# A one-core attention and FFN kernel: 64-row shift transposes at a unit's head, V tiles in first blocks, and a last chunk in three tiles and one

## The chip, the core and the metric

The kernel runs on one core of a Trainium2 chip. The metric is the device time of one execution in microseconds, the median of several runs; before the change it is 2961.74 us (three runs, 2959.02 to 2964.38).

## The reference

The input x has shape [2, 2048, 256] in float32. Attention and FFN each have a norm on both sides, and each is of the form x + layernorm(layer(layernorm(x))):

```python
x = x + _layernorm(_L0_attn_ref(_layernorm(x), Wq, bq, Wk, bk, Wv, bv, Wo, bo, gamma, beta))
x = x + _layernorm(_L0_ffn_ref(_layernorm(x), w_gate, w_up, w_down))
```

`_L0_attn_ref` is 16-head attention with 64 elements a head: projections with biases, softmax(q k / 8) v, an output projection with bias, the residual, and a layer norm with gamma and beta. `_L0_ffn_ref` has integer weights scaled by 1/127: silu(x Wg) * (x Wu), 768 hidden elements, and then the product with Wd.

## The kernel before, in words

**Units.** Attention is cut into 64 units (b, p, c): batch b of 2, head pair p of 8, block c of 512 queries of 4. `run_unit` runs one of them, in two blocks j = 0 and 1 of eight key tiles (128 keys each). For each key tile it issues the pair of products that gives the scores' maxima of the *next* unit (`max_pair`, L625, and DVE's reduction L632), and then the scores of this one (`scores`, L663): three pairs of float32r products (high by high, high by low, low by high) and a fourth pair, `unit` by `SH[u]`, that subtracts the row's shift; ScalarE takes the exponential (L664). Each head of the pair uses 64 rows of the array, so the shape of these products is 64\*128 (rows by columns) and they come in pairs. After a block follow the output projection of the unit before (`wo_half`, L252, with DVE's accumulation L263), POOL's and DVE's sums of the exponentials (`add_up`, L674 to L684), side jobs, and the eight PV steps (`pv`, L694), whose shape is 128\*64. In block 0 `sum_up` (L199) and the copy `first_half` (L223) come behind; then SyncE moves the row sums with eight small transfers (`few`, L208).

**The shift.** `shift_min` (DVE, L635) leaves the minima of the next unit's maxima in `n8`, columns 0 and 64. `shift_row` (L639) transposes its four 128x128 tiles on TensorE (L643) and ScalarE copies the result to `SH` (L645). In the kernel before, `run_unit` calls `shift_row(ahead)` behind block 1's PV steps; `cs_item(u)` follows it: DVE adds the two PV halves to `cf` (L230), ScalarE copies it to the high part of `cs` (L232), and POOL takes the low part (L233).

**What sets the order.** TensorE, DVE, ScalarE and POOL run in the order in which the program issues (`manual_schedule`); SyncE's transfers are ordered by the framework's scheduler. Side jobs are generators: `items(g)` says which begin in which block, and `advance` moves each one step when its kind, "R" (before PV's side work) or "F" (side work on TensorE), comes up. Before the change, "R" and "F" come up in both blocks. F jobs are the projections (`projs`, L578), V tiles (`v_tile`, L603, 24 products and a DVE add L613), weight preparation in batch 0 (`prep_jobs`, transposes L340), x transposes for batch 1 (`next_x`, `x_item`, L553 to L558), and the head jobs in batch 1 that turn finished attention rows of batch 0 into FFN input (`head_job`, L278 to L323, transposes L315).

**Buffers.** PSUM has two double buffers with tag "t" (`double()`: scores, projections, V, transposes, `wo_half`) and two with tag "x" (maxima and PV). There are 9 buffers for exponentials and 5 for V tiles.

**FFN.** Eight chunks of 512 rows, six hidden blocks each (`gate_up`, L961 to L983). A slot is one `gate_up` and one step of each waiting job: `end_job` (down products L995 of the chunk before, its norm and output), `own_job` (the norms of batch 1's rows), `x_out` (transposes L955 and the split L186, L187 of the next chunk, for chunks 4 to 7), and `last_units` (what attention left open). `finish` ends the last chunk.

Of the kernel before, what the change touches and what calls it, by code (L numbers as in the profile page):

```python
# [16 lines left out]
P = 128  # L17
# [11 lines left out]
def kernel(  # L29
# [112 lines left out]
    def x_chunk(b, c):  # L142
        return x_like(x, b, c)
# [83 lines left out]
    def cs_item(u):  # L227

        f = op.tile([P, QB], F32, tag="cf", name="cf")
        nc.vector.tensor_tensor(f, pvs.pop(u)[:, 0, :], raws.pop(u), ALU.add)  # L230
        t = op.tile([P, 2, QB], F32R, tag="cs", name="cs", bufs=2)
        nc.scalar.copy(t[:, 0], f)  # L232
        nc.gpsimd.tensor_tensor(t[:, 1], f, f32(t[:, 0]), ALU.subtract)  # L233
        ctxs[u] = t
# [92 lines left out]
    def prep_jobs():  # L327
        jobs = []

        def piece(w, dst, o, i0):  # L330
            src = hd.tile([P, TT, D], F32, tag="hx", name="wi")[:, 0, :].bitcast(I32)
            nc.sync.dma_start(out=src, in_=w[o * P : (o + 1) * P, i0 * P : (i0 + 2) * P])
            yield "R"
            f = hd.tile([P, TT, D], F32, tag="hy", name="wf")[:, 0, :]
            nc.scalar.copy(f, src)
            yield "F"
            yield "F"
            ps = double()[:, 0, :]
            for i in range(2):
                nc.tensor.transpose(ps[:, i * P : (i + 1) * P], f[:, i * P : (i + 1) * P], ident)  # L340
            t = hd.tile([P, TT, D], F32, tag="ht", name="wt")[:, :2, :].bitcast(F32R)
            split(t, ps[:, : 2 * P])
            for k in range(2):
                nc.sync.dma_start(
                    out=dst[:, k, i0 : i0 + 2, o * P : (o + 1) * P],
                    in_=f32(t[:, k, :]).rearrange("p (i n) -> p i n", i=2),
                )

        for w, dst, no, ni in (
            (w_gate, wg_dram, HC, DC),  # L350
            (w_up, wu_dram, HC, DC),
            (w_down, wd_dram, DC, HC),
        ):
            for o in range(no):
                for i0 in range(0, ni, 2):
                    jobs.append(piece(w, dst, o, i0))
        return jobs
# [87 lines left out]
    with ExitStack() as actx:  # L445
# [113 lines left out]

        def next_x(b, c):  # L560

            t = x_load(b, c)
            yield "R"
            x_norm(b, c, t)
            yield "F"
            x_item(c, t)
# [71 lines left out]

        def shift_row(u):  # L639

            ps = double()[:, 0, :]
            for qt in range(QT):
                nc.tensor.transpose(ps[:, qt * P : (qt + 1) * P], n8[:, qt, :], ident)  # L643
            SH[u] = bw.tile([P, QB], F32R, tag="sh", name="sh", bufs=2)
            nc.scalar.copy(SH[u], ps)  # L645

        def scores(u, kt):

# [55 lines left out]
        def items(g):  # L704

            b, p, c = units[g]
            at = {}

            def put(j, kind, f, *a, late=False):
                at.setdefault((j, kind), []).append((late, lambda: f(*a)))  # L710

            def now(j, f, *a):


                def job():
                    f(*a)
                    yield from ()

                put(j, "F", job)

            left = len(units) - g
            if p == 0:
                put(0, "R", next_acc, b, c)
            if b == 0 and p and (c != 2 or p == 1) and prep:
                put(0, "R", lambda: prep.pop(0), late=True)
            if b == 1 and 4 * p + c in (5, 11, 17, 23):
                put(0, "R", head_job, 0, (5, 11, 17, 23).index(4 * p + c), nc.gpsimd, late=True)
            if left == 3:
                put(1, "R", load_ffn, 0)
            if left == 2:  # L730
                put(0, "R", load_ffn, 1)
                put(1, "R", load_ffn, 2)
            if left == 1:
                put(0, "R", load_ffn, 3)
            if left == 2:
                put(1, "R", ahead, late=True)
            if b == 0 and p == 0:

                put(0, "R", x_stats_item, 1, c, late=True)


            want = [(0, *units[g + 2])] if left > 2 else []
            nb, npair = (b, p + 1) if p + 1 < NP else (b + 1, 0)
            if nb < B:
                same = nb == b
                want += [
                    (1, nb, npair, i)
                    for i in {1: (0,) if same else (), 2: (1,) if same else (0, 1), 3: (2, 3)}.get(c, ())
                ]
            for i in range(0, len(want), 2):  # L750
                now(0, projs, *want[i : i + 2])
            if c == 0 and p % 2 == 0:

                if g:
                    now(0, v_tile, b, p // 2, 3)
            if nb == B:
                return at
            if c == 0:
                put(0, "R", load_w, 1, nb, npair)
            if c == 1:  # L760
                put(0, "R", load_w, 0, nb, npair)
            if c == 2:
                put(0, "R", load_wo, nb, npair)
            if nb != b and c < 2:
                put(0, "R", next_x, nb, 2 * c)
                put(1, "R", next_x, nb, 2 * c + 1)
            if npair % 2 == 0:
                pg = npair // 2
                if c == 0:
                    put(1, "R", load_wv, nb, pg)  # L770
                if c == 2:
                    now(1, v_tile, nb, pg, 0)
                if c == 3:
                    now(1, v_tile, nb, pg, 1)
                    now(1, v_tile, nb, pg, 2)
            return at

        def begin():
# [64 lines left out]
            maxima(15, 16)  # L843
            shift_min(first)
            v_tile(0, 0, 3, True)
            shift_row(first)
            drain(load_wo(0, 0))

        ahead_job = own_job(OWN)
# [1 line left out]
        def ahead():  # L851
            for _ in ahead_job:
                yield "R"

        running = []

        def advance(kind, new):
# [9 lines left out]

        def run_unit(g, u):
            at = items(g)
            ahead = units[g + 1] if g + 1 < len(units) else None  # L870
            behind = units[g - 1] if g else None
            for j in range(2):
                for i in range(8):
                    if ahead and i < 7:
                        max_pair(ahead, 8 * j + i)
                    scores(u, 8 * j + i)
                if ahead:
                    max_pair(ahead, 8 * j + 7)
                if j == 1:
                    if ahead:  # L880
                        shift_min(ahead)
                    if behind:
                        inv_item(behind)


                if j == 1 and behind:
                    wo_half(behind, 0)
                if j == 0 and g > 1:
                    wo_half(units[g - 2], 1)
                adding = add_up(u, j)  # L890
                next(adding, None)
                advance("R", at.get((j, "R"), []))
                if j == 0:
                    advance("F", at.get((j, "F"), []))
                for i in range(8):
                    pv(u, 8 * j + i)
                if j == 0:
                    if behind:
                        sum_up(behind, pvs[u][:, 1, :])
                    first_half(u, behind)  # L900
                else:
                    if ahead:
                        shift_row(ahead)
                    cs_item(u)
                    drain(adding)
                    advance("F", at.get((j, "F"), []))

        with tc.manual_schedule(engines={EV.PE, EV.DVE, EV.Activation, EV.Pool}):
            begin()
# [135 lines left out]

    def finish(ch):

        mv = end_mv()
        for i in range(TT):
            down(ch, i, range(HC - 1))  # L1050
        for i in range(TT):
            down(ch, i, range(HC - 1, HC))
            end_stats(ch, i, mv)
        ready = end_rstd(mv)
        for i in range(0, TT, 2):
            end_out(ch, i, *ready, nc.vector)

    def last_units():

        wo_half(units[-2], 1)  # L1060
        yield
        ps = bank()
        sum_up(last, ps)
        row = op.tile([P, 2, QB], F32, tag="rr", name="rr")[:, 0, :]
        nc.scalar.copy(row, ps)
        sum_rows(last, row)
        for _ in range(3):
            yield
        inv_item(last)
        yield  # L1070
        wo_half(last, 0)
        yield
        wo_half(last, 1)

# [7 lines left out]
    with tc.manual_schedule(engines={EV.PE, EV.DVE, EV.Activation, EV.Pool}):  # L1082
        ffn_load(0)
        ffn_load(1)
        for ch in range(len(chunks)):
            for hc in range(HC):
# [5 lines left out]
                    jobs.append(own_job(OWN_AT[n]))  # L1092
                if ch > 0 and hc == 1:
                    jobs.insert(0, end_job(ch - 1))
                if hc == 3 and OWN <= ch + 1 < len(chunks):
                    jobs.append(x_out(ch + 1))
                for j in list(jobs):
                    if next(j, j) is j:
# [54 lines left out]
```

## Time and profile before

| | before |
|---|---|
| median of three runs | 2961.74 us |
| the profiled execution | 2966.69 us |
| its span, first to last instruction | 2964.9 us |
| mean granted TensorE clock | 0.995 |
| POOL's sums of exponentials, L677 | 636 x 2546 ns |
| DVE's maxima, L632 | 1024 x 1225 ns |
| exponentials, L664 | 1024 x 1027 ns |
| shift transposes, L643 | 256 x 286 ns (median 273) |
| shift copies, L645 | 64 x 588 ns |
| cs: DVE's add L230, ScalarE's copy L232, POOL's subtraction L233 | medians 692, 622, 1294 ns |

In the profile's rows the first number is the start in us from the span's start, then the length, the engine, the line, the operation, the tiles written and read, the shape (for TensorE first the part of the array that is used, rows\*columns) and the count. In brackets stands the idle time before, and what ended it. Matmul records overlap each other, since the array is pipelined, so that the step from one start to the next says more than the length of a record. The name s stands for both maxima and PV, t for every tile of the tag "t".

### The profile page before, as it was taken

To read this page: it belongs to the slowest core of one execution; us is meant where nothing else is said; L and a number is where in the kernel's file an instruction comes from. 1 tells how busy PE (TensorE), PEld (TensorE's weight loads), DVE (VectorE), ACT (ScalarE), POOL (GpSimd) and SP (SyncE) were. 2 spreads that over 40 slices of the span, in tenths; PEclk is the share of its full clock that TensorE was granted. 3 is DMA by queue.
4 is the path that set the end of the run, shared out by engine and by line. 5 is a ranking of instruction groups with operands and counts; after the bars stand their busy time and mean duration, and the time that the engine had idled before them with its cause. 6 is when DMAs were issued, how large, how long until landed. Compare 5 with 4: busy or idle time off the path is not lost.

```text
span 2964.9 us, 48241 instructions
## 1 busy us (share of the span) xinstructions
PE 2891.5 (98%) x19236; PEld 1749.7 (59%) x19236; DVE 2081.5 (70%) x2689; ACT 1466.1 (49%) x1740; POOL 2442.2 (82%) x1396
## 2 busy tenths in 40 slices
PE   7999999999999999999999999999999999999998
PEld 5555565556555565556555655555555565555887
DVE  6776677776777767776777777776777667774663
ACT  4545444554455444554555545454545445554443
POOL 4999878887888878887899988899799889988553
PEclk9999999999999999999999999999999999999999
DMA  2000000000000000010000001001000000112000
GB/s 59 19 12 12 13 12 12 10 17 5 15 12 13 10 12 24 5 42 10 26 21 10 7 10 33 5 13 31 5 7 24 20 1 10 44 58 72 29 29 29
DMA packets 125394, 59.10 MB, mean 20 GB/s; under 512 B 77200, under 2 KB 118416, under 8 KB 124784
## 3 DMA queue, kind: packets, MB, share of 16 engines
q1 hardware_dynamic: 124960, 55.62, 7.0%
q8 instruction: 150, 2.46, 0.3%
q0 software_dynamic: 208, 0.40, 0.1%
q14 instruction: 76, 0.62, 0.1%
HBM read 37.89 MB, written 17.83 MB: 19 GB/s over the span
## 4 chain that ended last, share of the span: by engine, by line
PE 83%; POOL 8%; DVE 4%; ACT 3%; issue 2%; DMA 1%; SPq 0%; ACTq 0%; POOLq 0%; DVEq 0%
PE t L663 29%; PE s L694 27%; PE s L625 8%; POOL accs L677 5%; PE t L578 5%; PE t L603 3%; ACT pt L664 2%; PE fp L995 2%; PE up L968 2%; PE gp L968 2%; PE s L199 2%; PE t L252 1%; PE t L643 1%; DVE nm L632 1%; POOL accs L684 1%
## 5 line engine op out<-in xcount | busy, mean ns | idle before, releaser
L677 POOL TENSOR_TENSOR accs<-accs,pt 128x1024 f32<-128x1024 f32 x636 | 1619.4, 2546 | 273.2 <-ACT pt L664 228.1
L632 DVE TENSOR_REDUCE nm<-s 128x2 f32<-128x1024 f32 x1024 | 1216.1, 1225 | 508.6 <-PE s L625 507.8
L664 ACT ACTIVATE pt<-t 128x1024 f32<-128x1024 f32 x1024 | 1050.0, 1027 | 258.6 <-PE t L663 188.0
L663 PE MATMUL t<-QN,KT 64*128 64x512 f32 x6144 | 915.5, 403 | 5.5 <-ACT pt L664 2.8
L694 PE MATMUL s<-pt,v 128*64 128x512 f32 x4096 | 907.1, 595 | 0.0
L663 PEld LDWEIGHTS t<-QN,KT 64*128 64x128 f32 x6144 | 522.6, 185 | 241.2 <-ACT pt L664 171.8
L694 PEld LDWEIGHTS s<-pt,v 128*64 128x64 f32 x4096 | 282.8, 137 | 538.1 <-issue 525.9
L625 PE MATMUL s<-KT,QN 64*128 64x512 f32 x2048 | 422.2, 409 | 6.5 <-DVE cf L230 3.7
L663 PE MATMUL t<-sh,unit 64*128 64x512 f32 x2048 | 405.5, 392 | 0.0
L684 POOL TENSOR_TENSOR accs<-accs,two 128x1024 f32<-128x1024 f32 x128 | 305.3, 2385 | 18.7 <-DVE two L683 7.7
L681 DVE TENSOR_TENSOR two<-pt 128x1024 f32<-128x1024 f32 x128 | 290.5, 2269 | 0.0
L625 PEld LDWEIGHTS s<-KT,QN 64*128 64x128 f32 x2048 | 192.1, 184 | 128.0 <-issue 61.1
L223 ACT COPY rr<-s 128x1024 f32<-128x1024 f32 x63 | 64.0, 1015 | 393.5 <-PE s L199 386.3
L645 ACT CAST sh<-t 128x512 fp32r<-128x512 f32 x64 | 37.6, 588 | 434.9 <-PE t L643 434.9
L263 DVE SCALAR_TENSOR_TENSOR acc<-t,rc,acc 128x256 f32<-128x256 f32 x500 | 206.9, 477 | 20.0 <-PE t L252 13.2
L663 PEld LDWEIGHTS t<-sh,unit 64*128 64x128 f32 x2048 | 193.4, 185 | 45.2 <-ACT sh L645 0.2
L674 POOL TENSOR_TENSOR accs<-pt 128x1024 f32<-128x1024 f32 x64 | 155.5, 2430 | 47.3 <-ACT pt L664 46.9
L578 PE MATMUL t<-xh,wqk 128*128 128x512 f32 x512 | 181.2, 414 | 12.5 <-ACT pt L664 10.5
L982 POOL TENSOR_TENSOR hT<-hf,hT 128x512 fp32r<-128x512 f32 x48 | 61.9, 1289 | 106.5 <-ACT hT L981 106.5
L578 PEld LDWEIGHTS t<-xh,wqk 128*128 128x128 f32 x512 | 97.7, 191 | 47.1 <-ACT pt L664 23.4
L588 ACT ACTIVATE QN<-t,bq_sb 128x512 fp32r<-128x512 f32 x64 | 44.0, 688 | 148.7 <-PE t L578 148.6
L252 PE MATMUL t<-wo,cs 64*128 64x256 f32 x1500 | 114.7, 285 | 1.6 <-ACT pt L664 1.5
(163 smaller groups left out, 2177.7 us busy)
## 6 DMA issues: line engine op xcount, KB each, us to landing
few<-rr SPq DMA_DIRECT2D x512, 0.5 KB, 2.0
xc<-in_L_attn_x_dram SPq DMA_DIRECT2D x8, 512.0 KB, 4.0
xT_dram<-hn SPq DMA_DIRECT2D x16, 256.0 KB, 2.2
out_dram<-o SPq DMA_DIRECT2D x16, 256.0 KB, 2.2
xT<-xT_dram SPq DMA_DIRECT2D x3, 1024.0 KB, 5.9
attn_dram<-acc SPq DMA_DIRECT2D x5, 512.0 KB, 2.6
acc<-in_L_attn_x_dram SPq DMA_DIRECT2D x4, 512.0 KB, 8.8
raw_w<-in_L_attn_Wq_dram SPq DMA_DIRECT2D x16, 128.0 KB, 2.2
```

The source lines that it names most:

```text
L252: nc.tensor.matmul(ps[e][:, i * D : (i + 1) * D], t[half(e), ci, s], w[half(e), wi, :], start=k == 0, stop=k == 2,)
L263: nc.vector.scalar_tensor_tensor(a, ps[e][:, i * D : (i + 1) * D], inv[:, e, q : q + 1], a, ALU.mult, ALU.add)
L578: nc.tensor.matmul(ps[:, k, :], w[:, wi, dc, :], xx[:, dc, s], start=n == 0, stop=n == 5)
L625: nc.tensor.matmul(s[:, e, :], QN[u][half(e), 0, qt * P : (qt + 1) * P], KT[b, p, kc][half(e), 0, :], start=True, stop=True,)
L632: nc.vector.tensor_reduce(nm[u][:, :, qt, kc : kc + 1], s, AX.X, ALU.max, negate=True)
L663: nc.tensor.matmul(ps[:, e, :], w, r, start=n == 0, stop=n == 3)
L664: nc.scalar.activation(pt, ps, AF.Exp, scale=QSCALE)
L674: nc.gpsimd.tensor_tensor(accs[u], todo[0], todo[1], ALU.add)
L677: nc.gpsimd.tensor_tensor(accs[u], accs[u], t, ALU.add)
L681: nc.vector.tensor_tensor(two, p8[n], p8[n + 1], ALU.add)
L684: nc.gpsimd.tensor_tensor(accs[u], accs[u], two, ALU.add)
L694: nc.tensor.matmul(pvs[u][half(e), 0, :], v[:, kt % 4, n : n + K], pt[:, e, :], start=kt % 8 == 0, stop=kt % 8 == 7,)
```

## The change

It has these parts.

1. `shift_row(u)` is called at the head of unit u and no longer behind the block before it. Each 128x128 transpose becomes two of 64 rows, one per half of `n8`'s partitions, which write 64 columns each in two banks; ScalarE's copy gathers from both.
2. `cs_item` stops after DVE's add. Its ScalarE copy and POOL subtraction are issued at the head of the next unit, behind the shift's copy. Behind the last unit they are issued at once.
3. "F" comes up in block 0 alone. V tile 0 of the next pair stays in unit c = 2, now in block 0; tiles 1 to 3 are made in block 0 of unit c = 0. Weight preparation loses one of its two "F" waits.
4. `next_x` gets a tile of its own for each of the chunks 0 to 2 (chunk 3 shares with 0), and chunk 1 begins in block 0 of its unit.
5. Head jobs 2 and 4 begin a unit earlier (11 to 10, 23 to 22).
6. FFN: `x_out` begins at hidden block 1 and not 3. In `last_units` the reciprocal and the first half of the projection come one slot earlier; the second half stays in its slot.
7. `finish` runs the first three tiles to their end, starts their norm, runs the fourth tile's 18 products, and writes four tiles of 128 rows each, not two of 256.

```diff
         nc.vector.tensor_tensor(f, pvs.pop(u)[:, 0, :], raws.pop(u), ALU.add)
+        yield
         t = op.tile([P, 2, QB], F32R, tag="cs", name="cs", bufs=2)
...
             nc.scalar.copy(f, src)
             yield "F"
-            yield "F"
...
-            t = x_load(b, c)
+            t = hd.tile([P, TT, D], F32, tag=("hx", "hy", "ht", "hx")[c], name="xc")
+            nc.sync.dma_start(out=t, in_=x_chunk(b, c))
...
-            ps = double()[:, 0, :]
+            ps = double()
             for qt in range(QT):
-                nc.tensor.transpose(ps[:, qt * P : (qt + 1) * P], n8[:, qt, :], ident)
+                for h in range(2):
+                    nc.tensor.transpose(
+                        ps[:, h, qt * K : (qt + 1) * K], n8[half(h), qt, :], ident[half(h), half(h)]
+                    )
             SH[u] = bw.tile([P, QB], F32R, tag="sh", name="sh", bufs=2)
-            nc.scalar.copy(SH[u], ps)
+            nc.scalar.copy(
+                SH[u].rearrange("p (q h r) -> p h q r", h=2, r=K),
+                ps[:, :, : QT * K].rearrange("p h (q r) -> p h q r", r=K),
+            )
...
-            if b == 1 and 4 * p + c in (5, 11, 17, 23):
-                put(0, "R", head_job, 0, (5, 11, 17, 23).index(4 * p + c), nc.gpsimd, late=True)
+            if b == 1 and 4 * p + c in (5, 10, 17, 22):
+                put(0, "R", head_job, 0, (5, 10, 17, 22).index(4 * p + c), nc.gpsimd, late=True)
...
-                if g:
-                    now(0, v_tile, b, p // 2, 3)
+                for i in range(1, 4) if g else ():
+                    now(v_tile, b, p // 2, i)
...
-                put(1, "R", next_x, nb, 2 * c + 1)
+                put(c, "R", next_x, nb, 2 * c + 1)
...
                 if c == 2:
-                    now(1, v_tile, nb, pg, 0)
-                if c == 3:
-                    now(1, v_tile, nb, pg, 1)
-                    now(1, v_tile, nb, pg, 2)
+                    now(v_tile, nb, pg, 0)
...
             at = items(g)
+            shift_row(u)
+            if cs:
+                drain(cs.pop())
...
-                    if ahead:
-                        shift_row(ahead)
-                    cs_item(u)
+                    cs.append(cs_item(u))
+                    next(cs[0])
+                    if u == last:
+                        drain(cs.pop())
                     drain(adding)
-                    advance("F", at.get((j, "F"), []))
...
-        mv = end_mv()
-        for i in range(TT):
-            down(ch, i, range(HC - 1))
-        for i in range(TT):
-            down(ch, i, range(HC - 1, HC))
-            end_stats(ch, i, mv)
-        ready = end_rstd(mv)
-        for i in range(0, TT, 2):
-            end_out(ch, i, *ready, nc.vector)
+        def end(tiles, eng):
+            mv = small["pool"].tile([P, TT, 2], F32, tag="mvo", name="mvo")
+            n = len(tiles)
+            for k, i in enumerate(tiles):
+                ln_stats([fp_tile(ch, i)], mv, k)
...
+            ln_rstd(rs, nb, mv[:, :n, :], n, LN_EPS, *chain())
+            yield
+            b, c = chunks[ch]
+            for k, i in enumerate(tiles):
+                o = fs.tile([P, D], F32, tag="oe", name="oe")
+                ln_apply(o, fp_tile(ch, i), rs[:, k : k + 1], nb[:, k : k + 1])
+                eng.tensor_tensor(o, o, x1s[ch][:, i, :], ALU.add)
+                nc.sync.dma_start(out=x_like(out, b, c)[:, i, :], in_=o)
+
+        for hcs in (range(HC - 1), range(HC - 1, HC)):
+            for i in range(3):
+                down(ch, i, hcs)
+        first = end((0, 1, 2), nc.gpsimd)
+        next(first)
+        down(ch, 3)
+        drain(first)
+        drain(end((3,), nc.vector))
...
         sum_rows(last, row)
-        for _ in range(3):
-            yield
+        yield
+        yield
         inv_item(last)
         yield
         wo_half(last, 0)
+        yield
         yield
         wo_half(last, 1)
...
-                if hc == 3 and OWN <= ch + 1 < len(chunks):
+                if hc == 1 and OWN <= ch + 1 < len(chunks):
                     jobs.append(x_out(ch + 1))
```

## The prediction

> **What bounds the kernel now.** First the page's busy times and chain, then the timeline of TensorE and ScalarE where one unit ends and the next begins, then the stretches where TensorE waits.
>
> ```profile
> PE 2891.5 (98%) x19236; PEld 1749.7 (59%) x19236; DVE 2081.5 (70%) x2689; ACT 1466.1 (49%) x1740; POOL 2442.2 (82%) x1396
> PE 83%; POOL 8%; DVE 4%; ACT 3%; issue 2%; DMA 1%; SPq 0%; ACTq 0%; POOLq 0%; DVEq 0%
> ```
>
> TensorE carries 83% of the chain, so a change is worth what it takes out of TensorE's stream. Since matmul records overlap, I count from start to start. The end of a unit:
>
> ```profile
> 965.90 7.09 PE L694 MATMUL s<-pt,v 128*64 128x512 f32 x32
> 972.92 0.66 PE L643 MATMUL t<-ident,n 128*128 128x128 f32 x4
> 973.51 0.50 PE L625 MATMUL s<-KT,QN 64*128 64x512 f32 x2
> 973.84 0.85 PE L663 MATMUL t<-QN,KT 64*128 64x512 f32 x6
> 974.53 0.40 PE L663 MATMUL t<-sh,unit 64*128 64x512 f32 x2
> ```
>
> ScalarE there (the copy of the shift, that of cs, the first exponential):
>
> ```profile
> 973.61 0.59 ACT L645 CAST sh<-t 128x512 fp32r<-128x512 f32 x1 [6.92 <-PE t L643]
> 974.10 0.62 ACT L232 CAST cs<-cf 128x512 fp32r<-128x512 f32 x1
> 975.03 1.03 ACT L664 ACTIVATE pt<-t 128x1024 f32<-128x1024 f32 x1 [0.31 <-PE t L663]
> ```
>
> In the middle of a unit there are no transposes between the 128\*64 products and the 64\*128 ones:
>
> ```profile
> 1038.95 1.03 PE L199 MATMUL s<-accs,ones 128*64 128x512 f32 x4
> 1039.90 0.49 PE L625 MATMUL s<-KT,QN 64*128 64x512 f32 x2
> 1040.24 0.86 PE L663 MATMUL t<-QN,KT 64*128 64x512 f32 x6
> ```
>
> The shape column gives the price of going from one array shape to another. In the trace's single records a PV pair follows another after 0.429 us; the first transpose comes 0.530 after the last PV pair (+0.10) and the second 0.166 after the first (then 0.109). From transposes to the max pair it is 0.202, to the first score pair another 0.335, where that step is 0.231 inside a stretch. Where transposes and next product share a shape (FFN, L955 to L968) the two steps sum to 0.345. So the second switch costs 0.202 + 0.335 - 0.345 = 0.19 us.
>
> **The pairs (64 units, 63 with a PV ahead).** Moving the transposes to the head of the next unit leaves TensorE's order as it was, except behind units with V tiles or x transposes. ScalarE's order is unchanged too: sh already stood ahead of cs. The real edit is the shape: 4 transposes of 128\*128 become 8 of 64\*128, the shape of the products behind. PV to transposes keeps its switch (as L199 to L625, 0.529); transposes to maxima loses its own.
>
> What eight cost instead of four no row shows: there is no fp32 64-row transpose. Ends: a pair steps at 0.055 (half the columns, half of 0.109), or its loads go one after the other, 0.218. The nearest row is the score pair of the same shape: its two weight loads start 3 ns apart, its matmuls too. The old step of 0.109 equals the gap between its 128-column loads, and the columns per load stay 128. I take 0.109 per pair, so four pairs last as long as four transposes. Against this stands a rule of the Trainium skill, "TensorEngine Tiling (Array Packing)", Instruction Overhead: a matmul costs some 60 cycles however few columns it has, and a dimension that is small already should not be split. Counted as eight such transposes in a row at the 0.109 shown, it gives 4 x 0.109 = 0.44 more per unit and a net loss of 0.25; by the score-pair row, a gain of 0.19. Concurrency of row halves is shown here, so I follow the row.
>
> Who is late next? The unit matmul waits for the sh copy. Counted from the last PV pair it starts at 2.137 now; the stream alone would bring it at 1.945. The copy starts 0.309 after the last transpose starts (0.26 with half the columns), takes 0.587, the load follows 0.05 later at best, the matmul 0.115 after that: 0.913 + 1.01 to 1.06 = 1.92 to 1.97. So at most 0.03 is given back. I take 0.17 per unit: **63 x 0.17 = -10.7 us**. The copy now reads two banks in 64-element runs; between 0.587 (same 512 elements) and 1.015 (rr, 1024 elements of two banks) I take the first. The cs copy behind it ends near 2.3, its POOL subtraction and the first exponential follow; that exponential waits for scores at 2.33. DVE's cf (0.69) stays ahead of the first maximum. The cover of cs is thus nearly gone, but not exceeded.
>
> **V in first blocks.** Same 24 products a tile, same DVE add (1.23). In a c=0 unit three tiles stand behind the Q projection; two buffers alternate, and each add has a tile's 2.85 us to be done in. DVE has 6 us idle there while PV runs, so 0; if that cover failed, up to 1.2 per tile. The removed second-block slot had also covered the sh copy; other units already live without it. prep loses one of two waits for a slot that is gone, and its transposes fall where they did; FFN weight loads advance a few slots later, still far ahead of the FFN.
>
> **Head jobs 11 to 10, 23 to 22.** Their transposes land in c=2 instead of c=3, where two projection calls had filled both buffers:
>
> ```profile
> 2040.98 0.39 PE L578 MATMUL t<-xh,wqk 128*128 128x512 f32 x1
> 2043.05 1.09 PE L315 MATMUL t<-ident,hy 128*128 128x128 f32 x8 [1.68 <-DVE KT L589]
> ```
>
> At c=2 there is one call, and in one case a V tile of 2.85 between. The step of 2.07 falls to about 0.2: **2 x -1.9 = -3.8** (to 0). Their SyncE transfers start a unit earlier, into the same free tiles.
>
> **next_x.** Separate tiles take the loads' wait for the previous transposes off SyncE's queue. But two x items now stand together ahead of projections, twice: the second waits for wo's buffer (DVE acc), the projections for DVE's xl behind acc and two (ends 2.5 us later than now). The second-block stall (1.07) and the transposes done early (0.9) offset most: +0.5 each, and half-clock risk; **+1.5** (-1 to +4).
>
> **x_out two slots earlier.** Now its second DVE split queues behind two norms of the slot:
>
> ```profile
> 2835.81 0.85 PE L968 MATMUL gp<-xT,fw 128*128 128x512 f32 x3
> 2838.66 0.73 PE L968 MATMUL gp<-xT,fw 128*128 128x512 f32 x2 [1.99 <-DVE xT L187]
> ```
>
> Four chunks begin so: 2.16, 2.16, 1.10, 1.10 over the usual step = 6.5 us. Two slots earlier the split is done before that queue forms; behind it hf is earlier by 0.66, and no other releaser is that late. **-6.0** (-6.5 to -2).
>
> **last_units.** One slot earlier for wo's first half. Its wait:
>
> ```profile
> 2758.22 0.58 PE L252 MATMUL fp<-wo,cs 64*128 64x256 f32 x1 [4.08 <-DVE acc L263]
> ```
>
> And the busy times of the 7 us after that wait (PE, PEld, DVE, ACT, POOL, then clock, DMA share, GB/s):
>
> ```profile
> 2757.00:2764.00 7.00, 5.57 (x22) 4.36 (x23) 6.49 (x26) 2.52 (x5) 6.21 (x5) 0.55 0.00 1
> ```
>
> DVE is busy 6.49 of 7 us, and the granted clock is 0.55. The 4.08 goes, but the next thing is late: the down products of chunk 0 need the banks that DVE frees behind a norm chain at 2763.2, some 0.8 earlier than now. TensorE then idles about 5 us there and may again get half clock after it. **+0.5** (-4 to +3).
>
> **finish.** Tile 3's 18 products cover the first norm chain (2.45 us). But the second chain follows it on DVE (2957 to 2959.5), and "oe" has two buffers for four tiles: tile 3's apply, and tile 2's ahead of it on ScalarE, wait for stores of tiles 0 and 1 (about 2.2 us to land). The last add ends near 2961.6, against 2961.45 now: **+0.2** (-1.2 to +1).
>
> Sum: -10.7 - 3.8 + 1.5 - 6.0 + 0.5 + 0.2 = **-18.3 us**. The profiled execution took 2966.69 (span 2964.9 and 1.8 around it), 4.95 over the median of the timed runs; it becomes 2948.4, and the median 2961.74 becomes **2943.4**.
>
> **Rivals.** (a) Loads of a pair are not concurrent: the last pair comes 0.33 later, the next product 0.44 later, the unit matmul 0.25 later than now: 63 x 0.25 = +15.8 in place of -10.7, in all 2961.7 + 8.2 = 2970, slower. It decides from a pair step of about 0.19 on, where the loss per unit reaches 0.12 and eats the 7.6 won elsewhere. For it: fp32 transposes in pairs appear nowhere; against it: score pairs at 3 ns. (b) The copy of 64-element runs takes about 0.76 instead of 0.587: the switch is saved and TensorE waits for sh instead; no gain at the boundary, 2954. For it: only 0.03 us of slack is left; against it: element count unchanged. (c) Pairs step at 0.055: another 0.15 per unit, 2934. For it: half the moving columns; against it: the load gap. (d) The boundary does nothing because POOL holds the pace (8% of the chain): gain only in the FFN and heads, 2954 as (b); TensorE's waits that trace to POOL are few (ScalarE waited for accs 6.5 us in all).
>
> **How the numbers follow.** Main case 0.62 (2937 to 2951); (b) with (d) 0.17; (c) 0.11; (a) 0.10. The SyncE order may also move stalls of 2 us with half clock after them (three such now), +-4. Range 2932 to 2958. About 0.2% (6 us) is what measuring can tell from no change: faster 0.84, same 0.07, slower 0.09.
>
> **What would show it.** After: 256 pairs (512 transposes), pair step 0.109, transposes to first score pair 0.345, sh copy 0.59, unit boundary 0.17 shorter; chunk starts 4 to 7 without the xT wait; L315 without the KT wait; the last units still with a bank wait near chunk 1. A boundary longer than before refutes the pairing, an xT wait still there refutes the FFN part.

## The result and the profile after

| | us | ratio to before, 95% interval |
|---|---|---|
| before, median of 12 runs beside it | 2961.72 (2958.76 to 2967.44) | |
| after, median of 12 runs | 2960.78 (2957.87 to 2963.76) | 0.9995 [0.9986, 1.0004] |
| forecast | 2943.4 (2932 to 2958) | |
| profiled execution: before / after | 2966.69 / 2961.08 | |

No change that can be measured, where 18 us had been forecast; the time lies above the range. The profiled execution of before was 5 us over its median. A second profile of the kernel before has a span of 2960.9, and its units have the same lengths within 0.07 us but for the start of the kernel (2.7 shorter) and units 6 and 4 (1.4 and 0.3 shorter). So I compare unit by unit and not by spans. A unit is counted from its shift transposes to those of the next.

The page's busy times and its chain, kernel after:

```profile
PE 2876.9 (97%) x19492; PEld 1742.6 (59%) x19492; DVE 2102.9 (71%) x2701; ACT 1467.1 (50%) x1740; POOL 2444.7 (83%) x1399
PE 85%; DVE 5%; POOL 4%; ACT 3%; issue 1%; DMA 1%; SPq 1%; ACTq 0%; DVEq 0%; POOLq 0%
```

TensorE is busy 14.6 us less than in the first profile of before and 10.7 less than in the second, but it is idle 82.4 us where it was idle 73.4 and 73.3. First the part that worked, the end of a unit on TensorE:

```profile
1097.92 1.89 PE L701 MATMUL s<-pt,v 128*64 128x512 f32 x8
1099.74 0.46 PE L645 MATMUL t<-ident,n 64*128 64x64 f32 x8
1100.01 0.47 PE L626 MATMUL s<-KT,QN 64*128 64x512 f32 x2
1100.33 0.86 PE L670 MATMUL t<-QN,KT 64*128 64x512 f32 x6
1101.03 0.39 PE L670 MATMUL t<-sh,unit 64*128 64x512 f32 x2
```

and on ScalarE:

```profile
1100.25 0.59 ACT L649 CAST sh<-t 128x512 fp32r<-128x512 f32 x1 [6.73 <-PE t L645]
1100.73 0.62 ACT L233 CAST cs<-cf 128x512 fp32r<-128x512 f32 x1
1101.52 2.19 ACT L671 ACTIVATE pt<-t 128x1024 f32<-128x1024 f32 x2 [0.17 <-PE t L670]
```

From the first transpose to the first score pair it is 0.59 us (1099.74 to 1100.33), before it was 0.92 (972.92 to 973.84); to the unit matmul 1.29, before 1.61. So a boundary is 0.32 to 0.33 shorter. In the single records the pairs start at 0, 0.113, 0.174 and 0.236, the two transposes of a pair 1 to 3 ns apart; before, the four transposes started at 0, 0.166, 0.275 and 0.384. So 0.15 comes from the pairs' own step of 0.061 and the rest from the switch: the maxima follow 0.035 after the last pair began, the scores 0.316 after them (0.202 and 0.335 before). The copy takes 588 ns at the median, as before. Over 63 boundaries that would be 20.8 us.

Now where TensorE waits, by releaser (us in all, times, longest). Kernel before, then kernel after:

```profile
PE gp L968 <- DVE xT L187: 5.9, 4, 2.0
PE t L578 <- DVE xl L558: 5.5, 4, 2.4
PE t L315 <- DVE KT L589: 3.4, 2, 1.7
PE t L340 <- DVE KT L589: 1.7, 1, 1.7
```

```profile
PE t L579 <- DVE xl L558: 10.2, 6, 2.8
PE fp L1002 <- DVE acc L264: 5.5, 1, 5.5
PE t L340 <- DVE KT L590: 5.2, 4, 2.2
PE misc L962 <- DVE xT L187: 5.0, 3, 2.6
PE s L626 <- DVE cf L230: 4.1, 4, 2.2
```

In all of these TensorE is held by a buffer that DVE has not freed or filled. The two largest entries, left out here, are ScalarE's and are as before (10.5 and 10.3 us in both kernels). Four places stand out. The x items of units 29 and 30 (transposes of x, then projections and a V tile):

```profile
1272.38 1.09 PE L553 MATMUL t<-ident,xc 128*128 128x128 f32 x8 [0.85 <-DVE acc L264]
1276.29 0.50 PE L579 MATMUL t<-xh,wqk 128*128 128x512 f32 x1 [2.83 <-DVE xl L558]
...
1322.04 0.79 PE L579 MATMUL t<-xh,wqk 128*128 128x512 f32 x1 [2.79 <-DVE xl L558]
...
1330.60 0.50 PE L604 MATMUL t<-wv,xh 128*128 128x256 f32 x2 [1.29 <-DVE KT L590]
```

Unit 29 went from 43.25 to 45.77 us, unit 30 from 46.07 to 54.03 (its successor is 3.29 shorter, since V tile 0 moved). Then unit 56 (c=0, three V tiles), 47.79 to 52.29, and the two c=2 units 14 and 46, on TensorE:

```profile
652.29 0.44 PE L340 MATMUL t<-ident,wf 128*128 128x128 f32 x2 [1.08 <-DVE KT L590]
...
1979.87 0.50 PE L626 MATMUL s<-KT,QN 64*128 64x512 f32 x2 [1.42 <-DVE cf L230]
...
1996.70 1.09 PE L316 MATMUL t<-ident,hy 128*128 128x128 f32 x8 [1.04 <-DVE KT L590]
...
2419.94 0.50 PE L604 MATMUL t<-wv,xh 128*128 128x256 f32 x2 [2.89 <-DVE QN L590]
```

What DVE did ahead of that QN in unit 56:

```profile
2413.81 3.30 DVE L688 TENSOR_TENSOR two<-pt 128x1024 f32<-128x1024 f32 x1
2417.03 0.42 DVE L96 BATCH_NORM_STATS2 bs<-hy 128x6 f32<-128x256 f32 x1
...
2419.16 0.72 DVE L590 SCALAR_TENSOR_TENSOR QN<-t,bq_sb,QN 128x512 fp32r<-128x512 f32 x1
```

Between 2417.03 and 2419.16 stand the second-norm statistics of the head job started at unit 54; ScalarE's part of QN was ready at 2414.40. Last, the FFN: the second projection of the last unit no longer waits, but the down products after it do; and the xT wait has left the chunk's start for the second transposes of x_out:

```profile
2758.05 4.08 PE L1002 MATMUL fp<-fw,hT 128*128 128x256 f32 x18 [5.54 <-DVE acc L264]
...
2847.75 1.12 PE L962 MATMUL misc<-ident,acc 128*128 128x128 f32 x4 [2.63 <-DVE xT L187]
```

After several of these waits TensorE gets half its clock. Busy times per stretch, then the granted clock, DMA share and GB/s:

```profile
1277.00:1280.40 3.40, 3.40 (x11) 1.34 (x11) 1.12 (x2) 0.69 (x1) 3.32 (x3) 0.50 0.00 0
...
1321.40:1328.20 6.80, 6.16 (x15) 4.81 (x16) 1.72 (x2) 0.64 (x1) 4.04 (x2) 0.50 0.43 145
...
2420.50:2423.90 3.40, 3.40 (x18) 3.40 (x17) 0.52 (x1) 0.00 (x0) 3.32 (x2) 0.50 0.00 0
2755.00:2761.80 6.80, 3.75 (x17) 3.75 (x18) 6.32 (x24) 1.28 (x3) 2.78 (x3) 0.50 0.00 0
2847.20:2850.60 3.40, 2.85 (x9) 2.47 (x10) 1.78 (x5) 2.08 (x4) 1.58 (x2) 0.50 0.00 0
```

In the first and third stretch TensorE works all the time. The V products of the third follow each other every 0.213 us in it and every 0.118 right after it, so such a stretch costs about 1.5 us (my estimate from these two steps) on top of its wait; the others begin within the wait.

### The profile page after: what moved, and what is told of

Read it like the earlier page. It is cut to its first block, busy times and chain, and to the rows that moved or that the text cites. A ratio compares the mean times of both kernels' runs of the same rounds, so it can differ in the third digit from the quotient of the medians.

```text
span 2959.3 us, 48771 instructions
## 1 busy us (share of the span) xinstructions
PE 2876.9 (97%) x19492; PEld 1742.6 (59%) x19492; DVE 2102.9 (71%) x2701; ACT 1467.1 (50%) x1740; POOL 2444.7 (83%) x1399
## 4 chain that ended last, share of the span: by engine, by line
PE 85%; DVE 5%; POOL 4%; ACT 3%; issue 1%; DMA 1%; SPq 1%; ACTq 0%; DVEq 0%; POOLq 0%
PE t L670 32%; PE s L701 28%; PE s L626 8%; PE t L579 5%; PE t L604 3%; POOL accs L684 2%; ACT pt L671 2%; PE fp L1002 2%; PE s L199 2%; PE gp L975 2%; PE up L975 2%; PE t L253 2%; DVE two L688 1%; DVE nm L633 1%; DVE acc L264 1%
## 5 line engine op out<-in xcount | busy, mean ns | idle before, releaser
L688 DVE TENSOR_TENSOR two<-pt 128x1024 f32<-128x1024 f32 x128 | 309.4, 2417 | 0.0
L579 PE MATMUL t<-xh,wqk 128*128 128x512 f32 x512 | 184.5, 421 | 18.2 <-ACT pt L671 10.5
```

Source lines behind the costliest of these rows:

```text
L579: nc.tensor.matmul(ps[:, k, :], w[:, wi, dc, :], xx[:, dc, s], start=n == 0, stop=n == 5)
L688: nc.vector.tensor_tensor(two, p8[n], p8[n + 1], ALU.add)
```

## The experiments

The theory that I formed from the two traces (Theory A where an expectation says so) is that the pairs earn what the unit shows, and that new waits at these few places give it back. Against it: the pairs earn little over the whole kernel, because ScalarE, DVE or POOL keep the pace; or one part costs in a place that I do not see. Times are medians, each beside runs of the kernel before on the same chip. These runs of before have medians of 2961.4 to 2962.6 us, so a difference between two changed kernels is sure to about 1 us.

**The pairs, alone and taken away.** First the pairs at the head with the split copy of cs, on the kernel before (V, heads, x items and FFN stay):

```diff
             at = items(g)
+            shift_row(u)
+            if cs:
+                drain(cs.pop())
...
-                    if ahead:
-                        shift_row(ahead)
-                    cs_item(u)
+                    cs.append(cs_item(u))
+                    next(cs[0])
```

> The kernel before with parts 1 and 2 alone: pairs of 64-row transposes at the unit's head and the late copy of cs; V tiles, x tiles, heads and FFN as before. Theory A (the pairs take 0.32 to 0.33 us out of each unit's TensorE stream, and the other parts gave it back as new waits): 2961.7 - 63 x 0.3 = about 2943, slightly less gained in the 24 units behind V or x work; unit boundaries 0.3 us shorter, FFN stage as before. Theory B (the shorter boundary is taken back elsewhere in the unit, since DVE or POOL holds the pace, so that no part was worth anything): 2958 to 2962.

Measured 2959.68, 0.9993 [0.9985, 1.0001]. A miss for the 20 us: plain boundaries are 0.33 shorter, as in the changed kernel, but where V tiles stay at the end of a unit the transposes now stand behind them. The three units around a V group gain little or nothing: those around units 14 and 22 come to +0.5 instead of -1.0. TensorE at the first boundary behind such a V tile:

```profile
675.73 0.46 PE L645 MATMUL t<-ident,n 64*128 64x64 f32 x8
676.87 0.96 PE L670 MATMUL t<-QN,KT 64*128 64x512 f32 x6 [0.39 <-ACT sh L649]
```

From transposes to scores it is 1.14 here, since the scores wait for ScalarE's copy of the shift; before, the V products stood between. Attention is 8 to 9 us shorter by the units, and 3.6 of that is lost in the FFN, where two chunk starts run at half clock in this profile and not in either profile of before.

Then the changed kernel with four 128-row transposes in place of the pairs, all else as changed:

```diff
-            ps = double()
+            ps = double()[:, 0, :]
             for qt in range(QT):
-                for h in range(2):
-                    nc.tensor.transpose(
-                        ps[:, h, qt * K : (qt + 1) * K], n8[half(h), qt, :], ident[half(h), half(h)]
-                    )
+                nc.tensor.transpose(ps[:, qt * P : (qt + 1) * P], n8[:, qt, :], ident)
```

> The changed kernel with the four 128-row transposes and the plain copy back, still at the head of the unit. Theory A: each boundary longer by 0.32 us, 2960.8 + 20 = 2981. Theory B: within 5 us of the changed kernel, 2961 to 2966.

Measured 2973.81, 1.0038 [1.0027, 1.0049]: 13.0 over the changed kernel. TensorE at a boundary of this kernel:

```profile
1104.90 0.66 PE L644 MATMUL t<-ident,n 128*128 128x128 f32 x4
1105.48 0.50 PE L626 MATMUL s<-KT,QN 64*128 64x512 f32 x2
1105.82 0.86 PE L664 MATMUL t<-QN,KT 64*128 64x512 f32 x6
```

0.92 again from transposes to scores. So the pairs are worth 13 us in the changed kernel, where neither expectation (20 or under 5) had it. By the units it is 14.6 and not 20.8: most units are 0.33 longer with four transposes, but 14 and 22 are the same, and 30, 46, 54 and 56, in which TensorE waits for DVE, are even 0.4 to 1.0 shorter.

**The x items.** The changed kernel with one x item in each of units 28 to 31, instead of two in two units:

```diff
-            if nb != b and c < 2:
-                put(0, "R", next_x, nb, 2 * c)
-                put(c, "R", next_x, nb, 2 * c + 1)
+            if b == 0 and 4 * p + c in (27, 28, 29, 30):
+                put(0, "R", next_x, 1, 4 * p + c - 27)
```

> The changed kernel, but one x item for batch 1 per unit (units 28 to 31, first blocks, each loaded a unit earlier) in place of two in unit 29 and two in unit 30. Theory A (two x items one behind the other wait for DVE through the two PSUM buffers, and TensorE then runs at half clock): units 28 to 31 together 6 to 9 us shorter, 2952 to 2955. Theory B (the profile's waits there are covered elsewhere): within 2 us of the changed kernel.

Measured 2953.76, 0.9971 [0.9962, 0.998], 7.0 less than the changed kernel. The four units take 172.5 us (changed 179.2; before 172.4). TensorE's waits there:

```profile
1233.38 0.50 PE L579 MATMUL t<-xh,wqk 128*128 128x512 f32 x1 [0.84 <-DVE acc L264]
...
1273.64 0.50 PE L579 MATMUL t<-xh,wqk 128*128 128x512 f32 x1 [0.85 <-DVE acc L264]
...
1317.87 0.50 PE L579 MATMUL t<-xh,wqk 128*128 128x512 f32 x1 [0.93 <-DVE xl L558]
1320.04 0.50 PE L604 MATMUL t<-wv,xh 128*128 128x256 f32 x2 [0.50 <-DVE KT L590]
```

No wait above 1 us and no half clock. So the cost was the two items together; the 1.3 us of four shorter boundaries is still given back to the waits of 0.8 to 0.9 that each unit keeps.

**The FFN of before under the changed attention** (x_out at hc 3, last_units and finish as before):

> The changed kernel with parts 6 and 7 undone: x_out at hidden block 3, last_units and finish of before. Theory A (the FFN parts only move their waits: the wait for a bank in chunk 1 in place of the one at wo, the wait at the transposes of x_out in place of the one at chunk starts): within 2 us of the changed kernel, 2959 to 2963. Theory B (the FFN parts did win their 5 us, and attention lost them): 2965 to 2967.

Measured 2963.34, 1.0008 [1.0, 1.0017], 2.6 over the changed kernel. So the FFN edits together earn 2.6, not 5.3; it lies between the two expectations. In this profile the FFN takes 238.0 us against 234.0 in before's and 234.6 in the changed kernel's: the same 2 us wait at a chunk's start is here followed by half clock, which it was not in before's. By the profiles of before the edits earned nothing.

**The heads.** The last head job from index 22 to 25 (unit 57):

```diff
-            if b == 1 and 4 * p + c in (5, 10, 17, 22):
+            if b == 1 and 4 * p + c in (5, 10, 17, 25):
```

> The changed kernel with the fourth head job begun three units later (25 in place of 22), so that its second norm's four statistics no longer stand on DVE ahead of the Q projection's low part in unit 56, where three V tiles follow. Theory A (that queue is what stops TensorE for 2.9 us there, with half clock behind it): unit 56 falls from 52.3 to 47.4 us, the whole to 2955 to 2957. Theory B (three V tiles in one block are too many for two PSUM buffers whatever DVE does): unit 56 stays above 50, the whole within 1.5 us of 2960.8.

Measured 2956.41, 0.9981 [0.9974, 0.9988], 4.4 less. Unit 56 is back at 47.28, and the only waits of TensorE in it are small:

```profile
2410.77 0.50 PE L579 MATMUL t<-xh,wqk 128*128 128x512 f32 x1 [0.17 <-ACT pt L671]
2412.71 0.50 PE L604 MATMUL t<-wv,xh 128*128 128x256 f32 x2 [0.28 <-DVE acc L264]
```

Unit 58 is 0.85 shorter, unit 61, where the transposes now fall, 1.96 longer.

**x_out's wait.** First its order in the slot, ahead of the other jobs instead of behind them:

```diff
-                    jobs.append(x_out(ch + 1))
+                    jobs.insert(0, x_out(ch + 1))
```

> The changed kernel with x_out put at the front of the slot's jobs, so that on DVE its split comes ahead of the norm chain of own_job. Theory A (the second transposes wait for a split that is queued behind that chain; so the FFN part was moved to the right slot but to the wrong place in it): the waits of 1.3, 2.8 and 1.5 us at the transposes go, chunks 3 to 6 together 5 us shorter, 2955 to 2957. Theory B (the chain itself then arrives late and TensorE waits for own rows or hT): within 1.5 us of 2960.8.

Measured 2961.87, 1.0001 [0.9992, 1.001]. A miss: three waits of 0.90, 2.45 and 2.42 remain. TensorE, then ScalarE of this kernel:

```profile
2836.16 0.60 PE L962 MATMUL misc<-ident,acc 128*128 128x128 f32 x4
...
2844.10 0.66 PE L962 MATMUL misc<-ident,acc 128*128 128x128 f32 x4 [2.45 <-DVE xT L187]
```

```profile
2840.82 0.59 ACT L984 ACTIVATE sg<-gp 128x512 f32<-128x512 f32 x1
2842.22 0.62 ACT L988 CAST hT<-hf 128x512 fp32r<-128x512 f32 x1 [0.81 <-DVE hf L986]
2842.74 0.58 ACT L186 CAST xT<-misc 128x512 fp32r<-128x512 f32 x1
```

The copy of the first half begins 6.0 us after its transposes have ended, right behind its own slot's sg and hT: ScalarE and DVE are a whole slot behind TensorE here (sg at 2840.82 belongs to the products that began at 2833.40). Each hT waits for DVE's hf; the hf before this one stands behind a norm chain on DVE, and the sg behind four steps of norms on ScalarE. Both halves use the one bank "misc", so the second transposes, one slot later, must wait. The order within the slot did not help; distance does:

```diff
             split(t[:, :, dc, :], ps)
             yield
+            yield
```

> The changed kernel; x_out's two halves are two slots apart instead of one. Theory: the second transposes wait because there is one bank for both halves and the first half's ScalarE copy stands behind the slot's hf and hT, so it comes a slot late; with two slots between, the waits of 1.3 to 2.8 us at chunks 4 to 6 go, FFN 234.6 to about 229, total about 2955 to 2957. Rival (the norm chains fill DVE through all slots of these chunks, so the split is as late as before): the second split is late for the next chunk's start as in the kernel before, FFN 233 to 235, no change.

Measured 2953.05, 0.9967 [0.9954, 0.9979], 7.7 less than the changed kernel; no wait at L962 is left, and the FFN takes 227.7 us instead of 234.6 (before: 234.0). Chunks 3 to 6 (counted from 0), in which x_out runs, take 104.0 us instead of 110.9; before it was 109.8. So the gain of some 6 us that was forecast for x_out is there once the halves stand apart.

**The last unit's second projection half, one slot earlier.**

```diff
         wo_half(last, 0)
         yield
-        yield
         wo_half(last, 1)
```

> The changed kernel with the last unit's second projection half one slot earlier (slot 5), so that DVE frees its banks ahead of the norm chain of slot 6. Theory A (the 5.5 us that TensorE waits at chunk 0's down products are that chain, with half clock behind it): the wait falls under 1.5 us, a new one of about 1.7 us comes at the second half itself; 2955 to 2957. Theory B (DVE is simply full in this stretch): the wait stays above 4 us and the time within 1.5 us of 2960.8.

Measured 2956.85, 0.9982 [0.9975, 0.9989], 3.9 less. The wait of 5.54 is gone; TensorE now waits at the projection itself:

```profile
2750.18 0.38 PE L253 MATMUL fp<-wo,cs 64*128 64x256 f32 x1 [1.88 <-DVE acc L264]
2750.96 1.65 PE L253 MATMUL fp<-wo,cs 64*128 64x256 f32 x11 [0.40 <-DVE acc L264]
```

**The kernel before once more** (the second profile named above):

> The kernel before, unchanged, profiled a second time. If the stalls of 2.1 us in unit 6, with half clock behind it, and the unthrottled chunk starts of the first profile are chance, they differ here: a span of about 2960 in place of 2964.9. If they belong to the kernel, they are here again at the same places.

Measured 2962.67, span 2960.9. The wait of 1.93 us in unit 6 is there again, but not the half clock behind it; the waits at the chunk starts are the same, at full clock.

**V's place, and the weight preparation's.** The kernel before with V in first blocks alone:

```diff
-                if g:
-                    now(0, v_tile, b, p // 2, 3)
+                for i in range(1, 4) if g else ():
+                    now(0, v_tile, b, p // 2, i)
...
-                    now(1, v_tile, nb, pg, 0)
-                if c == 3:
-                    now(1, v_tile, nb, pg, 1)
-                    now(1, v_tile, nb, pg, 2)
+                    now(0, v_tile, nb, pg, 0)
```

> The kernel before with one part of the change alone: V tiles in first blocks (tile 0 at c=2, tiles 1 to 3 at c=0 of the next pair), transposes, heads, x items and FFN as before. The prediction's theory (DVE's idle time in the first half covers the adds): 0, 2961.7 within 2. Placement theory: the three V groups of batch 0 lose about 1 us each (prep transposes behind V tile 0 wait for KT), those of batch 1 gain nothing, and the unit with three tiles in front of a head job's statistics may add 2 to 4: 2964 to 2968.

Measured 2966.88, 1.0016 [1.001, 1.0023]: 4.5 slower by this edit alone. Against the second profile of before, the groups around units 14 and 22 become 0.4 and 0.7 us longer and the one around unit 30 3.2 longer; those of batch 1 become 0.0, 0.3 and 1.7 shorter (the last I did not follow up). In unit 30 V tile 0 now stands behind an x item and the projections:

```profile
1333.93 0.50 PE L603 MATMUL t<-wv,xh 128*128 128x256 f32 x2 [1.67 <-DVE KT L589]
```

Attention is 2.6 longer by the units, and the FFN of this profile 2.7 longer, more than half of it in one chunk that is 1.6 longer than in before. So 2.6 of the 4.5 is seen in attention; whether the FFN's part comes from V stays open.

The preparation's transposes out of V's way (start at c=2 instead of c=1 in odd pairs, so that they fall at c=3):

```diff
-            if b == 0 and p and (c != 2 or p == 1) and prep:
+            if b == 0 and p and (c != (1 if p % 2 else 2) or p == 1) and prep:
```

> The changed kernel; a weight-preparation job no longer starts at c=1 of odd pairs but at c=2, so that its two transposes fall at c=3 and not behind V tile 0 in the three-buffer queue at c=2. Placement theory (the gain of the pairs is given back where V tiles, head jobs and prep transposes meet in two PSUM buffers): units 14, 22 and 30 lose the wait for DVE's KT of about 1.1 us each in front of the prep transposes, V groups of batch 0 become 1 to 1.3 us shorter like those of batch 1, in all -2 to -4 us: about 2958. Rival (POOL or DVE sets the pace in these units anyway): the wait moves to the next reader of the buffer, no change, 2960.8 within 1.

Measured 2964.41, 1.0009 [1.0001, 1.0018], 3.6 over the changed kernel: a miss with the wrong sign. Units 14 and 22 do become 1.5 shorter, but units 15 and 23 become 2.9 and 4.3 longer, for at c=3 two projection calls hold both buffers:

```profile
691.36 0.44 PE L340 MATMUL t<-ident,wf 128*128 128x128 f32 x2 [2.48 <-DVE KT L590]
```

**All together.** Four placements on the changed kernel (x items, heads at 25, the last projection half, the preparation):

> The changed kernel with four placements together: one x item per unit at 27 to 30, head jobs at 5, 10, 17, 25, the last unit's second projection half one slot earlier, prep at c=2 instead of c=1 in odd pairs. If the parts add: 2960.8 - 7.0 - 4.4 - 3.9 - 3 = 2942.5, and attention's unit boundaries then give what 63 x 0.33 says. Rival (half of what is won is clock recovered from the same few stretches, so that parts overlap): 2947 to 2951.

Measured 2947.23, 0.995 [0.9938, 0.9963], where the rival had 2947 to 2951. The same with x_out's halves apart:

> The four placements of the run before it, and x_out's halves two slots apart. If all parts add: about 2938 to 2940. If x_out's wait only moves: as the run before it, within 1.5 us.

Measured 2944.94, 0.9931 [0.9918, 0.9945], between its two expectations. And without the preparation's move, which had cost time alone:

> The changed kernel with x items one per unit at 27 to 30, head jobs at 5, 10, 17, 25, the last unit's second projection half one slot earlier and x_out's halves two slots apart; the weight preparation stays where the change has it, since moving it alone cost 3.6 us (its transposes then waited 2.6 us for DVE's KT at c=3). If that cost was also inside the four-placement kernel (2944.9): 2941 to 2942.5. If in that kernel it was hidden by another wait: 2944 to 2946.

Measured 2940.62, 0.9926 [0.9913, 0.994]: so the preparation's move had cost 4.3 us there too. It is the fastest of all, 21.8 us below the kernel before beside it. Its busy times and chain:

```profile
PE 2863.7 (98%) x19492; PEld 1732.5 (59%) x19492; DVE 2103.6 (72%) x2701; ACT 1469.2 (50%) x1740; POOL 2443.8 (83%) x1399
...
PE 86%; DVE 5%; POOL 4%; ACT 2%; issue 1%; DMA 1%; SPq 1%; ACTq 0%; DVEq 0%; POOLq 0%
```

TensorE's busy time fell by 13.2 us more, although its instructions are the same ones. Most of that is half clock that is gone: between 65 and 2920 us TensorE worked 23.0 us at half clock in the changed kernel and none here. From the changed kernel to this one the parts sum to 7.0 + 4.4 + 3.9 + 7.7 = 23.0, and 20.2 is measured.

## Why the prediction was wrong, step by step

The pairs were forecast at -10.7 and everything else at -7.6. With four whole transposes in place of the pairs the changed kernel measured 2973.81, 12.3 above the kernel before beside it. So everything else cost about 12 us, and the pairs' 13.0 just paid for it. The step that failed is therefore the terms of the moved side jobs: V was put at nothing, and the heads and x_out were put at their old wait alone, without asking what waits at the new place, and the two x items were put at 1.5 where they cost several times that.

| step of the sum | forecast | shown, timed |
|---|---|---|
| pairs | -10.7 | -13.0 in the changed kernel |
| V in first blocks | 0 | +4.5 alone on before |
| next_x | +1.5 | +7.0 against one item per unit |
| heads | -3.8 | +4.4 against 25 in place of 22 |
| x_out, last_units, finish | -5.3 | -2.6 |
| sum | -18.3 | +0.3 (measured: -0.9) |

The right column is not a strict partition: the x items and heads are measured against another place, not against before's own (the heads at 11 and 23 and `finish` alone were not run), and V and x meet in unit 30. That it closes within 2 us is in part luck. The units of the two traces give a second account. 63 boundaries at -0.33 are -20.8; beyond that, units 29 to 32 take back 8.0, units 54 to 56 6.0, the groups around units 14 and 22 1.0 each, 46 to 48 0.7, and units 58 and 59 earn 2.2. With small rests attention comes to 4.8 us less, and the FFN to 0.5 more. The start of the kernel differs by up to 3 us among the profiles, which is more than these sums miss.

- **The pairs**: mechanism right, size off in the other direction. "I take 0.109 per pair": it is 0.061, the rival (c) had 0.055; the score-pair row was the right one for the start within a pair (1 to 3 ns), and the loads follow at 0.061 too. Transposes to first score is 0.35 from the last pair, as forecast. With the switch that is 0.33 per boundary, not 0.17; the kernel gets only 13 us of the 20.8, since some units wait for DVE anyway. Rival (a), loads one after the other, and (b), a slower copy, are refuted by the records (0.061 and 588 ns). Rival (d) is refuted by the pairs' 13 us. The rule set beside this step (the Trainium skill, "TensorEngine Tiling (Array Packing)", Instruction Overhead: do not take a tiling factor from a dimension that is small already) came to 0.44 longer as I counted it there; the records make it 0.15 shorter.
- **V in first blocks, put at 0,** failed: alone it cost 4.5 us. I asked whether DVE has time for V's adds and not which other user stands in the line for the two buffers: the preparation's transposes behind V tile 0 (1.08 at 652.29), V behind x items and projections in unit 30 (1.67).
- **"2 x -1.9" for the heads** failed twice. At c=2 of unit 46 the head's transposes still wait (1.04 for KT), since a V tile stands between; its statistics delay cf there (1.42). And I followed a moved job's transposes but not its later steps: the statistics of the job begun at unit 54 fall in unit 56, ahead of the QN for which the second V tile waits (2.89, then half clock). Units 46 and 47 together went from 87.48 to 87.63, where two boundaries alone should have taken 0.66 off. Only the other pair earned: units 58 and 59 went from 84.54 to 81.71.
- **next_x, "+0.5 each, and half-clock risk"**: right mechanism, size off: one item per unit is 7.0 us faster. The two waits for xl (2.83 and 2.79) came as described, but half clock came with both of them, for 3.4 and 6.8 us.
- **x_out, "no other releaser is that late"** failed. The wait at chunk starts is gone as forecast; in its place the second half's transposes wait 1.1 to 2.6 us for the bank of the first. Two slots earlier the halves stand where ScalarE and DVE lag by a slot behind the norm chains. With the halves apart the forecast size came.
- **last_units, "the next thing is late"** was right: the down products wait 5.54 and get half clock. **finish**: the last chunk is 1.8 us shorter, of which the moved xT wait is 1.1; so about -0.7 in place of +0.2.

The only slower case among the rivals was the price of the pairs. That a kernel with this many jobs slotted by hand loses in queues for two buffers was no rival; the "+-4" stood for SyncE's order. The profile of before already had the signs (KT at L315, xl at L578, xT at L968).

## What to carry to other kernels

When jobs are moved among slots, list for every slot who uses the rotating buffers, in order, and who on DVE frees them; a job's later steps (statistics, copies) move too and can land in the worst unit. Two users of one bank need the distance by which the freeing engines lag behind TensorE, not an order within a slot. A saving on the bounding engine is real only where the next thing is not already waiting; test each placement alone, for here four of them (x items, heads, last projection, x_out's halves) hid 20 us.

## What was not expected of the hardware

- 64-row transposes in the two halves of the array step at 0.061 us a pair, weight loads included, against 0.109 for one 128-row transpose: from the first start to the last it is 0.24 for four pairs and 0.38 for four whole ones. The longer second step after the products (0.057 over the usual) is still there (0.052).
- TensorE at half clock after waits in mid-kernel came in stretches of 3.4 or 6.8 us, once behind a wait of only 1.78 (before, at 2322.67). It is not the same from run to run: the waits of 2.0 us at chunk starts had full clock in two profiles of before, and half clock at some of them in three other kernels with the same FFN code (the pairs alone, the FFN of before, V alone).
